# Window attention with one group of 49 tokens per matmul, smaller array tiles and a pair of accumulator banks

## The chip, the cores and the metric

The kernel runs on one core of a Trainium2 chip. A core has five engines with their own instruction streams: TensorE (matrix products; PE in the profile, its weight loads PEld), VectorE (DVE), ScalarE (ACT), GpSimd (POOL) and SyncE (SP, which issues the DMAs here). They meet through semaphores alone. TensorE writes into PSUM, eight banks of 512 fp32 numbers on each of 128 partitions; ScalarE and VectorE carry results from there to SBUF, the working memory. The metric is the device time of one execution in microseconds.

## The reference, cut to what matters

Four layers run over 32 images of 56 x 56 x 96: a conditional convolution block, a 5x5 depthwise convolution with a residual, a 3x3 depthwise with a pointwise convolution and batch norm, and a Swin block (window attention and an MLP). The change touches the attention of the last:

```python
shifted = jnp.roll(x, (-SHIFT, -SHIFT), axis=(1, 2))      # SHIFT = 3
win = _window_partition(shifted)                          # windows of 7 x 7 = 49 tokens
h = _layernorm(win, ln1_g, ln1_b)
q = (h @ wq).reshape(-1, L, NH, d)                        # L = 49, NH = 3, d = 32
k = (h @ wk).reshape(-1, L, NH, d)
v = (h @ wv).reshape(-1, L, NH, d)
attn = jnp.einsum('nqhd,nkhd->nhqk', q, k) / jnp.sqrt(jnp.float32(d))
attn = attn.reshape(B, nW, NH, L, L) + mask[None, :, None]
attn = jax.nn.softmax(attn, axis=-1).reshape(B * nW, NH, L, L)
out = jnp.einsum('nhqk,nkhd->nqhd', attn, v).reshape(-1, L, C)
```

Everything is fp32.

## The kernel before

An image passes four stages: router, conditional, depthwise and swin. Four images are in flight, one in each stage, so that the engines work on different stages side by side. The stages don't issue instructions; they record pieces of work with a `Recorder` (`call`, L292; several calls that must follow each other directly are put in one piece with `together`, L283). `order` (L339) then plays the pieces through a list scheduler: each engine has a queue sorted by a target time, a piece starts when what it needs is done and its buffers are free, and the function `cost` (L165) says how long it takes. `PLAN` and `interleave` (L1486) give the targets. The order found this way is written out, engine by engine, and every engine works through its list in that order. On the hardware nothing of the costs is left but this order. All recorded instructions carry the line L500 in the profile, since `give` issues them there.

A `Ring` (L194) is a set of equal buffers. The eight PSUM banks are one ring, `mm`, shared by all stages; a piece that needs a new bank waits in the plan until one is free, and a bank is free again when its last user is done. Where TensorE has nothing ready, `order` puts in an idle matmul, `ident` times `ident` (L1504).

In the swin stage an image is cut into 8 rows of windows, of 7 lines x 56 columns = 392 tokens each, that is 8 windows. Two windows that lie side by side make a pack, so a row has `NP` = 4 packs. `kT` and the normalized tokens have 64 columns (`SLOT`) for each window, 49 of them filled; the two windows of a pack lie on partitions 0 to 48 and 64 to 112 once tokens are on partitions, `PS` = 113 rows in all. For row i the loop near L1437 does:

- `exponentials` (L1130): scores of a pack, transposed (keys on partitions), are one product for each head, of 32 x 113 keys with 98 queries. Each head has its own bank and its own 32 rows of the array. All 113 x 98 scores of a pack come out; only the two 49 x 49 blocks on the diagonal belong to one window. ScalarE takes exp of those blocks, one instruction for each head and window of a pack (all four packs at once), into `exps`, whose other blocks were set to zero at the start (L703).
- `kept` (L1159): GpSimd multiplies by 0 or 1 where the shifted windows hold unrelated regions: the last window of a row, and all windows in the last row.
- `averaged` (L1174): sums of the exponentials with a stationary matrix of ones (`ones32`), three products of 113 rows with 392 columns into one bank, one head on each 32 columns of the array; then the products with `v`, one for each pack and head, into a second bank. ScalarE takes Ln of the sums and exp(-Ln) for the reciprocal.
- `divided` (L1202): VectorE refines the reciprocal with one Newton step and multiplies it with the averages. `attended` (L1274) projects the result and adds it to the residual.

The loop runs with a lag: scores of row i stand beside the sums of row i - 1 and the projection of row i - 2. A second version of the kernel for large scores (`general`) stands behind a branch that isn't taken with these inputs.

Of the kernel before, what the change touches and what calls it, by code (L numbers as in the profile page):

```python
# [14 lines left out]
ALU = mybir.AluOpType  # L15
# [149 lines left out]
def cost(engine, method, args, kw):  # L165
    if method == "preload_act_table_set":
        return 1300
    out = kw["out"] if "out" in kw else args[0]
    n = math.prod(out.shape[1:])
    if engine == "tensor":  # L170
        if method == "transpose":
            return 127
        k, m = args[1].shape[0], math.prod(args[1].shape[1:])
        if k == 32 and m == 32:
            return 68 * n / 392
        if k == 32:
            return 86
        if m == 32:
            return 75 if n < 128 else 255
        return 195 if n < 128 else 80 + 1.6 * n  # L180
    if len(args) > 3 and args[3] == ALU.pow:
        return 200 + 200 * n
    fixed, each = COST[engine, method]
    if engine == "scalar":
        if kw.get("accum_out") is not None:
            fixed += 190
        if hasattr(kw.get("scale"), "shape"):
            each += 0.37 if hasattr(kw.get("bias"), "shape") else 0.23
        elif hasattr(kw.get("bias"), "shape"):
            each += 0.25  # L190
    return fixed + each * n


class Ring:  # L194


    def __init__(self, tiles, banks=False):
        self.tiles, self.banks = tiles, banks
        self.free = [(0.0, n) for n in range(len(tiles))]
        self.made = self.begun = 0  # L200


class Buffer:


    def __init__(self, ring):
        self.ring = ring
        self.number = ring.made
        ring.made += 1
        self.slot = None  # L210
        self.users = {}
        self.state = {}
        self.owner = None


class View:
# [25 lines left out]
        return View(self.buffer, self.shown, self.path, parts)  # L242

    def found(self):
        t = self.buffer.ring.tiles[self.buffer.slot]
        for name, args, kw in self.path:
            t = getattr(t, name)(*args, **kw)
        return t
# [12 lines left out]
class Recorder:  # L261
# [23 lines left out]
        yield  # L285
        self.open = None

    def new(self, ring):
        b = Buffer(ring)
        return View(b, ring.tiles[0])  # L290

    def call(self, engine, method, args, kw, reads=(), writes=()):  # L292
        marks = (kw.pop("reads", ()), kw.pop("writes", ()))
# [45 lines left out]
    def order(self):  # L339
# [26 lines left out]
        def available(w):  # L366
            need = {}
            for b in w.needs:
                if b.slot is None:
                    need.setdefault(b.ring, []).append(b.number)  # L370
            return all(
                len(n) <= len(ring.free) and (ring.banks or max(n) < ring.begun + len(n)) for ring, n in need.items()
            )

        running = {}

# [11 lines left out]
        def done(w, now):  # L388
            for b in w.uses:
                b.left -= 1  # L390
                if not b.left:
                    b.ring.free.append((now, b.slot))
            for v in w.after:
                v.waits -= 1
                lag = 0 if v.engine == w.engine else TO_TENSOR[w.engine] if v.engine == "tensor" else CROSSING
                v.ready = max(v.ready, now + lag)
                if not v.waits:
                    ready.append(v)
# [6 lines left out]

        def begin(w):
            nonlocal count
            for b in w.needs:
                if b.slot is None:
                    b.ring.free.sort()  # L410
                    b.slot = b.ring.free.pop(0)[1]
                    b.ring.begun += 1
            result.append(w)
            w.start = now
            e = w.engine
            if e == "gpsimd" or e == "vector" and w.calls[0][0] == "scalar_tensor_tensor":
                running[e] = {"work": w, "left": w.ns, "since": now, "rate": 1.0}
                share(now)
                return
            free[e] = now + w.ns  # L420
            heapq.heappush(events, (free[e], count, None))
            heapq.heappush(events, (free[e] + w.landing, count + 1, w))
            count += 2
            if e == "tensor":
                heapq.heappush(events, (free[e] + SPARE_AFTER, count, None))
                count += 1
# [77 lines left out]
def kernel(  # L504
# [10 lines left out]
    def ring(name, shape, n):  # L515
        return Ring([const.tile(shape, F32, name=f"{name}{k}") for k in range(n)])

    def banks(name, n):
        return Ring([psum.tile([P, 512], F32, name=f"{name}{k}") for k in range(n)], banks=True)

    mm = cv = banks("banks", 8)
    xTs = ring("xT", [C, H * W], 2)
    h2s = ring("h2", [P, NB, STRIP * W], 2)
    wmixs = ring("wmix", [C, M], 2)
# [164 lines left out]
    else:  # L689
# [2 lines left out]

        slots = ring("slots", [C, NWIN, SLOT], 3)

        exps = ring("exps", [P, NH, NP, PK], 2)
        ones32 = const.tile([P, HD], F32, name="ones32")

    def first_others():
        for t, src in held:
            nc.sync.dma_start(out=t, in_=src)  # L700
        if not general:
            for t in slots.tiles + kTs.tiles + exps.tiles:
                nc.gpsimd.memset(t, 0.0)  # L703
            nc.gpsimd.memset(ones32, 1.0)

# [371 lines left out]
    def stage_swin(b, res):  # L1077
# [52 lines left out]
        def exponentials(i):  # L1130
# [2 lines left out]
            pss = [chip.new(mm) for _ in range(NH)]  # L1133
            with chip.together():
                for j in range(NP):
                    for h in range(NH):
                        hs = slice(h * HD, (h + 1) * HD)
                        chip.tensor.matmul(
                            pss[h][:PS, j * PK : (j + 1) * PK],
                            kT[hs, 2 * SLOT * j : 2 * SLOT * j + PS],  # L1140
                            qT[hs, j * PK : (j + 1) * PK],
                            start=True,
                            stop=True,
                        )
            e = exps_of[i] = chip.new(exps)
            for h in range(NH):
                for at in range(2):
                    ks, qs = slice(SLOT * at, SLOT * at + WT), slice(WT * at, WT * at + WT)
                    chip.scalar.activation(
                        e[ks, h, :, qs].part((h, at)),  # L1150
                        pss[h][ks, :RT].rearrange("k (j q) -> k j q", j=NP)[:, :, qs],
                        AF.Exp,
                        scale=1.0 / math.sqrt(HD),
                        reads=(tables,),
                    )

        every = [(h, at) for h in range(NH) for at in range(2)]

        def kept(i):  # L1159
            e = exps_of[i]  # L1160
            if i < NROW - 1:
                ks = slice(SLOT, PS)
                view = e[ks, :, NP - 1, WT:].part(*((h, 1) for h in range(NH)))
                chip.gpsimd.tensor_tensor(
                    view, view, keep_column[ks, None, :].to_broadcast([WT, NH, WT]), ALU.mult
                )
                return
            for at in range(2):
                ks = slice(SLOT * at, SLOT * at + WT)
                for h in range(NH):  # L1170
                    view = e[ks, h, :, WT * at : WT * at + WT].part((h, at))
                    chip.gpsimd.tensor_tensor(view, view, keep_last[ks], ALU.mult)

        def averaged(i):  # L1174

            v = rows_of.pop(i)[2]
            e = exps_of.pop(i).part(*every)
            pd = chip.new(mm)
            with chip.together():
                for h in range(NH):  # L1180
                    chip.tensor.matmul(
                        pd[h * HD : (h + 1) * HD, :RT],
                        ones32[:PS],
                        e[:PS, h].rearrange("k j q -> k (j q)"),
                        start=True,
                        stop=True,
                    )
            po = chip.new(mm)
            with chip.together():
                for j in range(NP):  # L1190
                    for h in range(NH):
                        hs = slice(h * HD, (h + 1) * HD)
                        chip.tensor.matmul(
                            po[hs, j * PK : (j + 1) * PK], v[:PS, j, hs], e[:PS, h, j], start=True, stop=True
                        )

            inv = chip.new(hids)[:C, :RT]
            chip.scalar.activation(inv, pd[:C, :RT], AF.Ln, reads=(tables,))
            chip.scalar.activation(inv, inv, AF.Exp, scale=-1.0, reads=(tables,))
            averages[i] = pd, po, inv  # L1200

        def divided(i):  # L1202

            pd, po, inv = averages.pop(i)
            step = chip.new(hids)[:C, :RT]
            chip.vector.tensor_tensor(step, pd[:C, :RT], inv, ALU.mult)
            chip.vector.scalar_tensor_tensor(step, step, 2.0, inv, ALU.subtract, ALU.mult)
            oT = output_of(i)
            chip.vector.tensor_tensor(
                oT[:C].rearrange("c (r n w) -> c r n w", n=NWIN, w=7),  # L1210
                by_windows(step),
                by_windows(po[:C, :RT]),
                ALU.mult,
            )

# [351 lines left out]
```

## Time and profile before

| | |
|---|---|
| time, median of 3 runs | 5202.46 us (5202.14 to 5204.24) |
| profiled execution, span | 5212.6 us |
| granted TensorE clock, mean | 0.985 |
| score matmuls, `banks<-qT,kT` 32x98 | 6144 records, 267.4 us busy |
| sums, `banks<-exps,ones` 113x392 | 1536 records, 221.7 us busy |
| averages, `banks<-exps,v` 113x98 | 6144 records, 221.9 us busy |
| POOL `exps<-exps,keep_column` 49x147 | 224 instructions, 925 ns each |
| DVE `hid<-banks,hid`, `hid<-hid,hid`, `oT<-hid,banks`, 96x392 | 256 each; 555, 637 and 551 ns |
| POOL `tb<-tb` 112x384 | 128 instructions, 1372 ns each |

The profile is of one execution, whose span is 0.2% over the median of the runs. A group is named by what it writes and reads, with partitions x elements; rows with a star give rows*columns of the array that a matmul uses. Each matmul call shows as two weight loads and two matmul records. Busy time of a group of matmuls is the union of overlapping records, so the mean of one record is much longer than its share of the time.

### The profile page before, as it was taken

Reading aid. Unit: us, or ns where it says so; the run is one execution under the profiler, and the core shown is the slowest. Engines: PE = TensorE matmul, PEld = TensorE weight load, DVE = VectorE, ACT = ScalarE, POOL = GpSimd, SP = SyncE. Lnnn points to the kernel's source line nnn. Section 1 sums busy time; section 2 is a strip of 40 time slices with the busy share of each in tenths; the row PEclk is TensorE's granted clock in tenths of the full one; section 3 lists DMA queues with packets and bytes.
Section 4 is the critical chain, followed back from the end, with each engine's and each line's share of the span. In section 5 each row is a group of like instructions: output and inputs, shape, how many; then the busy total and the mean of one; then the engine's idle time right before and its main releaser. Section 6 shows DMA issues by size and latency. Waiting matters only on the chain.

```text
span 5212.6 us, 139630 instructions
## 1 busy us (share of the span) xinstructions
PE 5050.6 (97%) x58578; PEld 3343.9 (64%) x58578; DVE 4300.9 (83%) x5561; ACT 3836.9 (74%) x7649; POOL 3028.8 (58%) x2432
## 2 busy tenths in 40 slices
PE   5789999999999999999999999999999999999999
PEld 4556666666666666666666666666666666666677
DVE  7877988888888888888888888888888888888722
ACT  3457778877778777777877777877777877777755
POOL 5455766565665556666555665656576555566533
PEclk9899999999999999999999999999999999999999
DMA  1111101111111111111111111111111111110110
GB/s 43 23 28 37 38 18 32 33 39 36 39 21 30 31 39 36 39 23 30 33 35 37 37 30 26 30 36 38 37 35 22 32 33 39 36 39 21 23 28 19
DMA packets 482577, 166.34 MB, mean 32 GB/s; under 512 B 477951, under 2 KB 478612, under 8 KB 478868
## 3 DMA queue, kind: packets, MB, share of 16 engines
q1 hardware_dynamic: 481940, 157.33, 14.8%
q8 instruction: 463, 7.59, 0.6%
q14 instruction: 174, 1.43, 0.1%
HBM read 41.60 MB, written 38.54 MB: 15 GB/s over the span
## 4 chain that ended last, share of the span: by engine, by line
PE 74%; POOL 10%; DVE 5%; ACT 5%; issue 4%; DMA 1%; SPq 0%; ACTq 0%; DVEq 0%; POOLq 0%
PE banks L500 74%; DVE h L500 3%; POOL tb L500 3%; POOL lnd L500 2%; POOL xT L500 2%; ACT exps L500 2%; POOL exps L500 2%; POOL var L500 1%; ACT hid L500 1%; ACT h L500 1%; DMA out<-tb 1%; DVE wmix L500 1%; DVE hid L500 1%; ACT slots L500 0%; DVE res L500 0%
## 5 line engine op out<-in xcount | busy, mean ns | idle before, releaser
L500 DVE SCALAR_TENSOR_TENSOR h<-h,mix,h 128x784 f32<-128x784 f32 x3072 | 3309.6, 1113 | 71.1 <-ACT h L500 54.0
L500 POOL TENSOR_TENSOR var<-var,mhalf 112x4 f32<-112x4 f32 (+1 forms) x512 | 775.2, 1519 | 426.3 <-DVE var L500 419.6
L500 PE MATMUL banks<-x,band 32*32 32x392 f32 x24576 | 856.3, 510 | 0.0
L500 POOL TENSOR_TENSOR xT<-y,xT 96x392 f32<-96x392 f32 x256 | 470.2, 1838 | 445.5 <-ACT y L500 444.1
L500 PE MATMUL banks<-xT,wmix 96*128 96x448 f32 (+1 forms) x1536 | 697.9, 553 | 0.5 <-DVE wmix L500 0.5
L500 ACT ACTIVATE h<-h,biasd,s 128x784 f32<-128x784 f32 x384 | 398.9, 1039 | 366.1 <-DVE h L500 366.0
L500 ACT ACTIVATE hid<-banks,c 128x448 f32<-128x448 f32 (+1 forms) x768 | 436.5, 582 | 288.3 <-PE banks L500 279.9
L500 POOL TENSOR_TENSOR tb<-res 112x384 f32<-112x384 f32 (+1 forms) x256 | 476.4, 1866 | 286.7 <-DMA out<-tb 196.7
L500 PEld LDWEIGHTS banks<-w,hid 128*112 128x112 f32 x5376 | 584.7, 183 | 82.0 <-issue 37.8
L500 PE MATMUL banks<-hT,w 96*128 96x448 f32 (+1 forms) x1536 | 615.6, 502 | 0.2 <-DVE tb L500 0.2
L500 POOL TENSOR_TENSOR lnd<-res,var 112x384 f32<-112x384 f32 (+1 forms) x512 | 594.8, 1168 | 32.8 <-PE banks L500 16.2
L500 ACT ACTIVATE h<-banks,bias,s 128x448 f32<-128x448 f32 (+1 forms) x768 | 538.6, 709 | 91.0 <-PE banks L500 85.4
L500 PE MATMUL banks<-w,hid 128*112 128x96 f32 x5376 | 593.1, 267 | 7.4 <-ACT hid L500 6.4
L500 PE MATMUL banks<-h,wmix 128*96 128x392 f32 x1536 | 557.7, 501 | 15.7 <-ACT h L500 15.7
L500 PEld LDWEIGHTS banks<-x,band 32*32 32x32 f32 x24576 | 404.7, 103 | 250.9 <-issue 165.9
L500 ACT ACTIVATE exps<-banks 49x196 f32<-49x196 f32 x1536 | 506.2, 330 | 40.2 <-PE banks L500 15.3
L500 POOL TENSOR_TENSOR exps<-exps,keep_column 49x147 f32<-49x147 f32 x224 | 207.1, 925 | 480.8 <-ACT exps L500 427.4
L500 PEld LDWEIGHTS banks<-h,wmix 128*96 128x96 f32 x1536 | 244.1, 165 | 256.8 <-issue 209.2
L500 PEld LDWEIGHTS banks<-xT,wmix 96*128 96x128 f32 x1536 | 261.2, 192 | 200.7 <-issue 95.5
L500 DVE TENSOR_REDUCE var<-lnsq 112x4 f32<-112x388 f32 (+1 forms) x512 | 253.1, 497 | 157.6 <-POOL lnd L500 118.1
L500 ACT ACTIVATE h<-h,mix 128x784 f32<-128x784 f32 x384 | 364.5, 949 | 18.0 <-POOL h L500 10.1
L500 PEld LDWEIGHTS banks<-hT,w 96*128 96x128 f32 x1536 | 256.4, 190 | 144.9 <-issue 74.8
(132 smaller groups left out, 7460.2 us busy)
## 6 DMA issues: line engine op xcount, KB each, us to landing
xT<-in_x SPq DMA_DIRECT2D x32, 1176.0 KB
x<-xT SPq DMA_DIRECT2D x384, 98.0 KB
out<-tb SPq DMA_DIRECT2D x128, 168.0 KB
filtered<-x SPq DMA_DIRECT2D x384, 49.0 KB
filtered<-x SPq DMA_DIRECT2D x384, 42.0 KB
out<-tb SPq DMA_DIRECT2D x128, 126.0 KB
filtered<-x SPq DMA_DIRECT2D x384, 7.0 KB
wpw<-in_L_conv_Wpw SPq DMA_DIRECT2D x1, 576.0 KB
```

The costliest lines, as they stand in the source:

```text
L500: getattr(getattr(self.nc, w.engine), method)(*args, **kw)
```

## The change

The scores and averages are made for one window at a time. Scores: the stationary operand is the 64 columns of `kT` of one window and one head, the moving one its 49 queries; the window's place in its pack, `at`, gives the half of the partitions that the result goes to. `exps` no longer has blocks that are never used: it is 128 partitions x 3 heads x 4 packs x 49, so exp is one instruction for each head over all 128 partitions (rows 49 to 63 and 113 to 127 hold what the zero columns of `kT` give). In the last row `kept` is one multiplication over all heads.

```diff
             with chip.together():
                 for j in range(NP):
-                    for h in range(NH):
-                        hs = slice(h * HD, (h + 1) * HD)
-                        chip.tensor.matmul(
-                            pss[h][:PS, j * PK : (j + 1) * PK],
-                            kT[hs, 2 * SLOT * j : 2 * SLOT * j + PS],
-                            qT[hs, j * PK : (j + 1) * PK],
+                    for at in range(2):
+                        n = 2 * j + at
+                        for h in range(NH):
+                            hs = slice(h * HD, (h + 1) * HD)
+                            chip.tensor.matmul(
+                                pss[h][SLOT * at : SLOT * (at + 1), j * WT : (j + 1) * WT],
+                                kT[hs, SLOT * n : SLOT * (n + 1)],
+                                qT[hs, WT * n : WT * (n + 1)],
...
             e = exps_of[i] = chip.new(exps)
             for h in range(NH):
-                for at in range(2):
...
+                chip.scalar.activation(
+                    e[:, h].rearrange("k j q -> k (j q)").part(h),
+                    pss[h][:, : NP * WT],
+                    AF.Exp,
...
+            keep = keep_last.rearrange("k j q -> k (j q)")
+            view = e.rearrange("k h j q -> k h (j q)")
+            chip.gpsimd.tensor_tensor(view, view, keep[:, None, :].to_broadcast([P, NH, NP * WT]), ALU.mult)
```

Sums and averages of a row go into one pair of neighbouring banks, one bank for each half of the partitions: columns 0 to 195 hold the sums, 256 to 451 the averages. All thirty products are one piece of work. Their outputs are written in the order line, pack, column, in runs of 7.

```diff
-            pd = chip.new(mm)
...
-            po = chip.new(mm)
...
+            both = chip.new(mm, pair=True)
+            halves = [slice(SLOT * at, SLOT * at + WT) for at in range(2)]
+            with chip.together():
+                for at, ks in enumerate(halves):
+                    for h in range(NH):
+                        chip.tensor.matmul(
+                            both[h * HD : (h + 1) * HD, at, : NP * WT].rearrange("c (r j w) -> c j r w", j=NP, w=7),
+                            ones32[ks],
+                            e[ks, h].rearrange("k j q -> k (j q)"),
...
                 for j in range(NP):
+                    for at, ks in enumerate(halves):
+                        for h in range(NH):
+                            hs = slice(h * HD, (h + 1) * HD)
+                            chip.tensor.matmul(
+                                both[hs, at, 256 : 256 + NP * WT].rearrange("c (r j w) -> c j r w", j=NP, w=7)[:, j],
+                                v[ks, j, hs],
+                                e[ks, h, j],
...
-            chip.scalar.activation(inv, pd[:C, :RT], AF.Ln, reads=(tables,))
+            chip.scalar.activation(inv, both[:C, :, : NP * WT], AF.Ln, reads=(tables,))
```

`divided` reads both banks in one instruction and puts the two halves side by side as it writes `oT`. The eight banks are now allocated as four tensors of two banks. The ring gives a pair only where an even bank and the next one are free together, gives single banks first from pairs that are already broken, and serves a pair ahead of single banks in the same piece. The memset of `exps` is gone.

```diff
+    def room(self, buffers):
+        twice = sum(b.pair for b in buffers)
+        if len(buffers) + twice > len(self.free):
+            return False
+        if twice and twice > len(self.halves()[1]):
+            return False
+        return self.banks or max(b.number for b in buffers) < self.begun + len(buffers)
...
+        slots = {n for _, n in self.free}
+        alone = [f for f in self.free if f[1] ^ 1 not in slots] if self.pairs else []
+        f = (alone or self.free)[0]
...
-    mm = cv = banks("banks", 8)
+    pairs = [psum.tile([P, 2, 512], F32, name=f"banks{k}") for k in range(4)]
+    mm = cv = Ring([pairs[k // 2][:, k % 2] for k in range(8)], banks=True, pairs=pairs)
```

`cost` gets planned times for the new products, in ns for a call:

```diff
+        if k == 32 and m == SLOT:
+            return 28
+        if k == WT:
+            return 24 if n == WT else 60
         if k == 32:
             return 86
         if m == 32:
-            return 75 if n < 128 else 255
+            return 75
```

## The prediction

> **What bounds the kernel now.** I read the page first (busy shares and the chain), then the table of two-image windows, then the groups with shapes kept apart, then one stretch of TensorE's timeline. The page:
>
> ```profile
> PE 5050.6 (97%) x58578; PEld 3343.9 (64%) x58578; DVE 4300.9 (83%) x5561; ACT 3836.9 (74%) x7649; POOL 3028.8 (58%) x2432
> ...
> PE   5789999999999999999999999999999999999999
> ...
> DVE  7877988888888888888888888888888888888722
> ...
> PE 74%; POOL 10%; DVE 5%; ACT 5%; issue 4%; DMA 1%; SPq 0%; ACTq 0%; DVEq 0%; POOLq 0%
> ```
>
> In the two rows of digits each digit is the busy tenths of a fortieth of the span. TensorE is busy nearly throughout, VectorE at eight to nine tenths until the last two slices, where only the last image's attention is left; and three quarters of the chain that ends last lie on it. A busy TensorE can hide waiting, because ends are modelled and because the plan puts in idle matmuls (`ident` times `ident`) where nothing is ready. So the steady part has to be looked at. The work repeats every 310 us, two images:
>
> ```profile
> core 0: us, PE busy (x) PEld busy (x) DVE busy (x) ACT busy (x) POOL busy (x), PEclk, DMA share, GB/s
> 1200.00:1510.00 310.00, 306.02 (x3595) 199.83 (x3595) 268.97 (x344) 238.91 (x478) 185.13 (x151) 0.99 0.16 33
> 2400.00:2710.00 310.00, 306.04 (x3596) 200.32 (x3594) 268.75 (x344) 238.89 (x478) 184.52 (x151) 0.99 0.16 33
> ```
>
> TensorE leaves 4 of 310 us free (2 us an image); VectorE leaves 41, ScalarE 71, GpSimd 125. In the window 600 to 4700 us, 26.5 images, the idle matmuls number few:
>
> ```profile
> L500 PE MATMUL banks<-ident 128*128 128x128 f32 x524 | 81.8, 283 | 0.0
> ```
>
> 524 records, about 119 ns from start to start, are 62 us or 2.4 us an image. So of 155 us for an image TensorE has 150 us of needed work, and saved TensorE time should shorten the period until VectorE (134 us an image) is full.
>
> One row (56 x 7 tokens, 8 rows an image, 256 in all) spends this on attention products; the columns are start and duration in us:
>
> ```profile
> 2526.69 1.04 PE L500 MATMUL banks<-qT,kT 32*113 32x98 f32 x24
> 2527.67 0.86 PE L500 MATMUL banks<-exps,ones 113*32 113x392 f32 x6
> 2528.35 0.86 PE L500 MATMUL banks<-exps,v 113*32 113x98 f32 x24
> 2529.14 0.53 PE L500 MATMUL banks<-wo,oT 97*112 97x97 f32 x3
> ```
>
> Start to start: scores 0.98, sums 0.68, averages 0.79, together 2.45 us. Each call appears as two records (fp32 passes). Three tiles, one per head, work side by side, so scores and averages are 8 rounds of three and the sums 2 rounds. The single records behind these rows show rounds starting 99.3 ns apart in the scores, 84.5 in the averages and 329 in the sums; inside a round, tiles start about 7 ns apart. 329/392 is 0.84 ns a column, and 98 columns of it are 82 of the 84.5: the averages and sums stream columns. The scores' 99.3 is more than 82; that is their weight load of 113 columns. What is left of a group (0.98 less 8 x 99.3, 0.79 less 8 x 84.5) is 0.19 and 0.11 us for filling and for the drain where the next group has another tile shape.
>
> **What the Trainium skill says.** "TensorEngine Tiling (Array Packing)", Tiling Modes: 32x64 gives 8 tiles, 64x32 also 8, tiles load and multiply in parallel, and a change of mode drains the engine. The trace agrees for 32x113, 113x32 and for 12 tiles of 32x32; the two new shapes are not in it. "TensorE: Matmul & The Clock Gate", LDWEIGHTS: a load costs its columns/1.2 ns, whatever the contraction. 113/1.2 is 94 ns beside the 99.3 ns round: agrees. The same page, "Wait — 56ns, not 53.3ns?": start-to-start never drops below about 25 ns. The 7 ns between tiles contradicts this within a burst; for a long run the fastest in the trace is 84.5/3 = 28 ns a pair, so it stays open. "PSUM — Partial Sum Buffer", Specifications: a non-contiguous output slows matmuls significantly. Every output before is contiguous, so no row shows it.
>
> **The change part by part.**
>
> Scores (L1130): 12 calls of 113x98 become 24 of 64x49, six tiles at once (three heads, two column halves), so still 8 rounds. A round is the larger of the load, 64/1.2 = 53 plus the 5 seen above = 58 ns, the stream 49 x 0.84 = 41, and six starts, 42. 8 x 58 + 0.19 = 0.65 us: saves 0.33.
>
> Sums (L1174): 3 calls over 392 columns become 6 over 196, six tiles at once (two row halves into two banks): 2 x 196 x 0.84 plus 0.02 = 0.35 us: saves 0.33.
>
> Averages: 12 calls become 24, 8 rounds of six. Load 32/1.2 = 27, stream 41 + 3, starts 42: I take 48 ns. 8 x 48 + 0.11 = 0.49: saves 0.30. Outputs of sums and averages now go out in runs of 7 words. I price this at nothing, since an fp32 pass writes only one element per 0.84 ns; the other end is a doubling, which takes back 0.33 and 0.35 and leaves the scores' 0.33.
>
> TensorE sum: I round 0.96 down to 0.88 us a row, for skew not seen in the trace. 256 x 0.88 = 225 us, 7.0 us an image. Ends: 0.96 x 256 = 246, and with slow scattered writes 0.28 x 256 = 72.
>
> ScalarE: six exponentials of 49x196 become three of 128x196.
>
> ```profile
> L500 ACT ACTIVATE exps<-banks 49x196 f32<-49x196 f32 x1536 | 506.2, 330 | 40.2 <-PE banks L500 15.3
> L500 POOL TENSOR_TENSOR exps<-exps,keep_last 49x196 f32<-49x196 f32 x192 | 170.2, 909 | 64.8 <-ACT exps L500 60.7
> L500 ACT ACTIVATE x<-banks 128x392 f32<-128x392 f32 x192 | 80.9, 494 | 27.1 <-PE banks L500 27.1
> L500 ACT ACTIVATE hid<-banks 96x392 f32<-96x392 f32 x256 | 126.3, 493 | 21.5 <-PE banks L500 17.9
> ```
>
> The last two rows: 128 and 96 partitions cost the same, so I keep 330 ns. 768 x 330 = 253 us leave ScalarE, 0.99 us a row, and the scores' three banks come free that much earlier.
>
> GpSimd: `kept` for a last row is one multiply of 128x588 for six of 909 ns. `tb<-tb` 112x384 takes 1372, so 588/384 of it is 2.1 us (ends 1.7 and 2.9): 3.4 us x 32 = 107 us less, on a wait that the sums sit behind. The other rows' 49x147 stays.
>
> VectorE: three operations a row at 392 elements stay (555, 637, 551 ns); only their patterns change. The last one already reads permuted runs of 7 at the price of the contiguous one, so nothing is added.
>
> Waits: the sums and averages become one unit, so Ln waits for all 30 calls. It began 0.68 us after the group's start and will begin about 0.84 after: 0.16 us on the path to the division, hidden behind other rows' ScalarE work; uncovered, it would cost 0.16 x 256 = 41 us. The bank of the sums is now held until the last VectorE operation, some 1.7 us longer (637 + 551 + Exp). And an even/odd pair of banks must be free at one moment; everything queued for a bank on TensorE can stand behind that. No DMA and nothing in SP's queue is changed. The planner's constants for the new calls change the order written out for all engines; I give that no value of its own, but an uncertainty below.
>
> Total: the period goes from 155 by at most 7.0 to 148; VectorE's 134 is then 91% of it, so VectorE is what is late next, and I take off a tenth: 6.3 us x 32 images = 202 us, and 3 us for the end, where the last image runs alone and its row chain is shorter by the exponentials. The profiled span is 5212.6 us and nothing lies around it in the times shown; their median 5202.46 is 0.998 of it. 5212.6 - 205 = 5007.6, x 0.998 = 4998 us.
>
> **The rivals.**
>
> A, forecast (0.64): 4998, own range 4945 to 5060.
>
> B, partial (0.24): another limit takes over early. Either scattered writes are slow (72 us of TensorE left) or pairs of banks come late and VectorE at 91% can't be kept fed, with idle matmuls growing from 2.4 to about 6 us an image. Then about 95 us remain: 5107, with 0.03 of the chance within 0.2% of before. For it: GpSimd and VectorE hold 15% of the chain. Against it: only 4 us of gaps in 310.
>
> C, slower (0.12): long runs of small tiles hit an issue floor. At the page's 25 ns a pair scores and averages take 96 x 25 = 2.4 us plus 0.3 for fill and drain plus 0.35 for the sums, 3.05 us against 2.45: +0.6 us x 256 = 154 us, 5356. It decides from (2.45 - 0.65)/96 = 19 ns a pair upward. For it: nothing in the trace runs faster than 28 ns a pair for long, and calls double. Against it: each rate seen is already explained by columns or loads, and six records in a burst start within 15 ns.
>
> That the tiles don't run in parallel at all would look like C, only stronger.
>
> **How the numbers follow.** The predicted time is A's. The range 4945 to 5130 holds A, most of B, and leaves out C and the ends. Taking 0.2% (10 us) as what can be told from no change: faster 0.85 (A and most of B), within it 0.03, slower 0.12.
>
> **What would show it.** Matmul records rise by 27 calls x 2 x 256 = 13824. Right: groups of 48 score records about 0.65 us start to start, 12 sum records 0.35, 48 average records 0.5; 768 exponentials at 330 ns; a two-image period near 297 us. Wrong for sizes: averages at 0.8 us (slow writes). C: 48 records at 1.2 us or more. B: small groups as forecast, but more `ident` records and gaps, the period above 303.

## The result, and the profile after

The changed kernel takes 6101.7 us (median of 4 runs, 6070.35 to 6122.49) against 5203.2 us of the kernel before on the same chip: ratio 1.172, 95% interval 1.1685 to 1.1758. 4998 was predicted. The profiled execution has a span of 6068.5 us at a mean granted clock of 0.951 (before: 5212.6 and 0.985).

The page of the changed kernel, the lines that answer to those shown of before:

```profile
PE 5354.7 (88%) x73354; PEld 3485.9 (57%) x73354; DVE 4245.9 (70%) x5561; ACT 3585.7 (59%) x6881; POOL 2892.8 (48%) x2270
...
PE   5788888898899899989888988889998899888898
...
DVE  7856867676777677677767677676766876777612
...
PE 44%; ACT 9%; DVE 5%; issue 3%; POOL 2%; DMA 0%; ACTq 0%; SPq 0%; DVEq 0%; POOLq 0%
```

ScalarE's work fell by 251 us and GpSimd's by 136, as meant, and yet each engine of the page is busy for a smaller share of the span. TensorE's row of digits has eights where it had nines from end to end. TensorE's busy time rose by 304 us although its work shrank, and its idle time rose from 162 to 714 us (span less busy).

Part of this is the clock. In the traces it is either full or half. It is half for 595 us of the changed kernel's profile and for 162 us of the one before, and TensorE is slower there: records of `banks<-h,wmix` start 653 ns apart at half clock and 329 elsewhere, in both. So up to 217 of the 898 us may be a slower TensorE (half of 433 us; an estimate, and an upper end, since TensorE doesn't set the pace everywhere). No run isolates what lowers the clock.

The two 310 us windows that held exactly two images before:

```profile
core 0: us, PE busy (x) PEld busy (x) DVE busy (x) ACT busy (x) POOL busy (x), PEclk, DMA share, GB/s
1200.00:1510.00 310.00, 281.29 (x4131) 176.22 (x4130) 227.62 (x287) 195.31 (x380) 154.36 (x121) 1.00 0.15 32
2400.00:2710.00 310.00, 274.82 (x3501) 182.97 (x3501) 223.05 (x288) 187.20 (x361) 158.38 (x122) 0.93 0.16 32
```

TensorE now leaves 29 and 35 us of 310 free, where it left 4. VectorE gets through 287 instructions in place of 344. The two windows are no longer alike: the strict repeat of two images is gone.

Were the new matmuls slower than thought? Two stretches of TensorE's timeline, start and duration in us, in brackets the idle time before and what ended it:

```profile
2545.12 0.90 PE L537 MATMUL banks<-slots,wq 96*96 96x392 f32 x2 [0.31 <-ACT h L537]
...
2583.58 0.77 PE L537 MATMUL banks<-qT,kT 32*64 32x49 f32 x48
2584.28 0.88 PE L537 MATMUL banks<-ident,lnd 112*96 112x112 f32 x7
2584.99 0.40 PE L537 MATMUL banks<-ident 128*128 128x128 f32 x2
2585.32 0.55 PE L537 MATMUL banks<-exps,ones 49*32 49x196 f32 x12
2585.68 0.66 PE L537 MATMUL banks<-exps,v 49*32 49x49 f32 x48
2586.27 0.59 PE L537 MATMUL banks<-ident,lnd 112*96 112x112 f32 x4
...
2588.56 0.90 PE L537 MATMUL banks<-slots,wq 96*96 96x392 f32 x2 [0.76 <-ACT h L537]
2589.94 0.90 PE L537 MATMUL banks<-slots,wk 96*96 96x392 f32 x2 [0.48 <-ACT exps L537]
```

They were not. Start to start, the scores take 0.70 us, the sums 0.36, the averages 0.59: 1.65 us against 2.45. What is new are the brackets, on projections to queries and keys. The profile says what ended a wait, not why it was waited for. The compiled program does: each instruction names the semaphore values that it waits for, and these can be traced back to the instruction that sets them. The last two lines wait until the bank that they write has been read by its last user; these are true waits, for a bank that comes late. The first line waits for an activation that reads the other bank of its tensor, and shares no data with it. Over 600 to 4700 us the table of TensorE's waits (total us, times, longest) had two lines before:

```profile
PE banks L500 <- POOL lnd L500: 44.3, 39, 2.8
PE banks L500 <- ACT hid L500: 6.4, 13, 0.5
```

Now it is much longer and begins with

```profile
PE banks L537 <- ACT h L537: 90.4, 120, 2.4
PE banks L537 <- ACT hid L537: 53.9, 80, 1.4
PE banks L537 <- ACT y L537: 33.0, 46, 2.2
PE banks L537 <- ACT res L537: 29.6, 44, 3.4
PE banks L537 <- ACT exps L537: 27.4, 59, 1.1
```

Many short waits; the largest totals are on ScalarE operations, which carry results out of banks. In the same window the idle matmuls, which were 524 records, are

```profile
L537 PE MATMUL banks<-ident 128*128 128x128 f32 x1144 | 200.7, 306 | 58.0 <-ACT h L537 20.9 <-DVE res L537 11.3 <-ACT slots L537 5.5
```

and the pieces that were to shrink on the other engines did:

```profile
L537 ACT ACTIVATE exps<-banks 128x196 f32<-128x196 f32 x768 | 211.0, 331 | 142.5 <-PE banks L537 129.7 <-POOL var L537 3.9 <-DVE res L537 3.2
...
L537 POOL TENSOR_TENSOR exps<-exps,keep_last 128x588 f32<-128x588 f32 x32 | 50.3, 1571 | 23.2 <-ACT exps L537 13.8 <-PE banks L537 9.5
```

So every local effect came, and the kernel lost 898 us. Two things had changed for the whole program besides the attention products: how the banks are allocated, and the order written out.

### The profile page after: what moved, and what is told of

It reads as the page before. It is cut to its first block, busy times and chain, and to the rows that moved or that the text cites. A ratio compares the mean times of both kernels' runs of the same rounds, so it can differ in the third digit from the quotient of the medians.

```text
span 6068.5 us, 167841 instructions
## 1 busy us (share of the span) xinstructions
PE 5354.7 (88%) x73354; PEld 3485.9 (57%) x73354; DVE 4245.9 (70%) x5561; ACT 3585.7 (59%) x6881; POOL 2892.8 (48%) x2270
## 4 chain that ended last, share of the span: by engine, by line
PE 44%; ACT 9%; DVE 5%; issue 3%; POOL 2%; DMA 0%; ACTq 0%; SPq 0%; DVEq 0%; POOLq 0%
PE banks L537 44%; DVE h L537 3%; ACT h L537 3%; ACT hid L537 2%; DVE hid L537 1%; DVE res L537 1%; POOL var L537 1%; ACT slots L537 1%; ACT exps L537 1%; ACT y L537 1%; POOL lnd L537 0%; ACT x L537 0%; DVE tb L537 0%; ACT res L537 0%; POOL tb L537 0%
## 5 line engine op out<-in xcount | busy, mean ns | idle before, releaser
L537 DVE SCALAR_TENSOR_TENSOR h<-h,mix,h 128x784 f32<-128x784 f32 x3072 | 3253.0, 1093 | 249.8 <-ACT h L537 236.2
L537 POOL TENSOR_TENSOR var<-var,mhalf 112x4 f32<-112x4 f32 (+1 forms) x512 | 825.3, 1616 | 792.7 <-DVE var L537 717.7
L537 PE MATMUL banks<-x,band 32*32 32x392 f32 x24576 | 885.4, 511 | 25.1 <-ACT h L537 10.2
L537 PE MATMUL banks<-xT,wmix 96*128 96x448 f32 (+1 forms) x1536 | 734.0, 578 | 72.1 <-ACT h L537 15.3
L537 PE MATMUL banks<-hT,w 96*128 96x448 f32 (+1 forms) x1536 | 646.1, 517 | 113.1 <-ACT hid L537 44.0
L537 PE MATMUL banks<-ident 128*128 128x128 f32 x2624 | 424.7, 300 | 149.2 <-ACT h L537 65.6
L537 POOL TENSOR_TENSOR tb<-res 112x384 f32<-112x384 f32 (+1 forms) x256 | 356.0, 1395 | 370.6 <-DMA out<-tb 274.6
L537 PEld LDWEIGHTS banks<-ident 128*128 128x128 f32 x2624 | 362.7, 204 | 245.3 <-ACT h L537 83.5
L537 DVE TENSOR_TENSOR tb<-banks,tb 112x384 f32<-112x384 f32 (+1 forms) x256 | 129.6, 506 | 469.6 <-PE banks L537 330.3
L537 DVE TENSOR_TENSOR hid<-banks,hid 96x392 f32<-96x392 f32 x256 | 142.6, 557 | 395.7 <-ACT hid L537 361.1
```

The lines of the kernel that those rows point to most:

```text
L537: getattr(getattr(self.nc, w.engine), method)(*args, **kw)
```

## The experiments

Times are medians; each ratio is against the kernel before on the same chip, with its 95% interval. "Single tensors" means eight tensors of one bank, as before; "wide tensors" four of two banks, as in the change.

### The tensors alone

The kernel before, same order, same bank numbers, same instructions, with one edit:

```diff
-        return Ring([psum.tile([P, 512], F32, name=f"{name}{k}") for k in range(n)], banks=True)
...
+    pairs = [psum.tile([P, 2, 512], F32, name=f"banks{k}") for k in range(4)]
+    mm = cv = Ring([pairs[k // 2][:, k % 2] for k in range(8)], banks=True)
```

> The kernel before with one edit: the eight banks are allocated as four tensors of two banks, as in the changed kernel; the planned order and every bank's number stay the same. Theory W (waits are drawn for a whole tensor, so a matmul into one bank also waits for readers and writers of its neighbour): far slower, 5700 to 6600 us, with TensorE gaps of several hundred us. Rival L (the choice of just-freed banks makes the waits): 5203 +- 10 us. Rival P (late pairs of banks): 5203 +- 10 us.

Measured: 5853.54 us, 1.1247 (1.1227 to 1.1267). No planned operation differs, nor does the bank of any, and 647 us are lost. Its page and its waits of TensorE:

```profile
PE 5362.9 (92%) x58578; PEld 3423.2 (58%) x58578; DVE 4254.7 (73%) x5561; ACT 3861.0 (66%) x7649; POOL 2936.3 (50%) x2432
```

```profile
PE banks L500 <- ACT exps L500: 46.0, 71, 1.2
PE banks L500 <- ACT h L500: 44.7, 58, 1.9
PE banks L500 <- ACT hid L500: 31.8, 53, 1.7
PE banks L500 <- ACT slots L500: 27.0, 46, 1.9
```

The same list of waits on ScalarE is here. The record counts are those of before (58578), yet busy time rose by 312 us, and idle time by 328. This profile is at half clock for 442 us in place of 162, which is up to 140 us of the busy time (an estimate); the rest may be waiting between a record that has begun and the next, which would count as busy, and is not separated here. The compiled programs show why TensorE waits. Its waits on ScalarE, traced back to the instruction that sets the semaphore:

```
kernel                               the other end uses
                                     the same bank   the other bank of the two
before                                    2662                0
before with wide tensors                   299             1945
changed kernel                             906             1106
changed kernel in single tensors          2481                0
```

Counted are the waits that a matmul carries itself; a wait for data that the matmul reads is not put into the second column. The last row is the program of the next run. The semaphores are drawn for a whole tensor. A matmul into one bank of a pair waits for whoever still reads the other bank, and the reader of one bank for a matmul that fills the other (1363 waits of ScalarE in the wide kernel, none before). These are false waits: no data is shared. With the program's waits laid over the profiles, matmuls that wait for the other bank alone have 328 of the 490 us of TensorE's idle time in front of them in the wide kernel, and 312 of the 714 us in the changed one. There another 247 us stand before matmuls that wait for their own bank alone (44 of 162 us before).

### The change with its waits made true

The changed kernel's own order and bank numbers, in single tensors. An instruction that spans the pair (logarithm, first and last division) is written out once for each bank:

```diff
-    pairs = [psum.tile([P, 2, 512], F32, name=f"banks{k}") for k in range(4)]
-    mm = cv = Ring([pairs[k // 2][:, k % 2] for k in range(8)], banks=True, pairs=pairs)
+    mm = cv = Ring([psum.tile([P, 512], F32, name=f"banks{k}") for k in range(8)], banks=True, pairs=[None])
...
+                    if w.engine != "tensor" and any(v.buffer.pair for v in views):
+                        for at in range(2):
```

> The changed kernel with its own planned order and bank numbers, but eight tensors of one bank; the three instructions that read both banks of a pair (Ln, first and last VectorE operation) are written out as two each, one for each bank, without the planner's knowledge (some 150 ns more on ScalarE and 300 ns on VectorE a row). Theory W (waits on the neighbour's bank): 5350 to 5550 us, the loss from 5203 to 6102 falls by more than half. If those waits don't matter in this order: 6100 us or more.

Measured: 5483.34 us, 1.0526 (1.0503 to 1.0549). 618 of the 898 us go with the false waits, although the split may itself cost something (below). And the changed kernel, still wide, with the rule dropped that gives a single bank from a broken pair first:

```diff
-        alone = [f for f in self.free if f[1] ^ 1 not in slots] if self.pairs else []
-        f = (alone or self.free)[0]
+        f = self.free[0]
```

> The changed kernel, four tensors of two banks and pairs, but a single bank is the longest free one, no longer one whose neighbour is in use. Theory W: still 5700 to 6100 us, since every bank has a neighbour to wait for. Rival L (the choice of banks makes the loss): 5400 us or less.

Measured: 5759.97 us, 1.1064 (1.1045 to 1.1082). 342 us better than the change, still wide: the rule hands out the neighbour of a bank in use, with which false waits are surest. This run also has a new order, so it is not as clean as the first. The rule alone, on the kernel before with its single tensors:

```diff
-                    b.slot = b.ring.free.pop(0)[1]
+                    slots = {n for _, n in b.ring.free}
+                    alone = [f for f in b.ring.free if f[1] ^ 1 not in slots] if b.ring.banks else []
+                    f = (alone or b.ring.free)[0]
```

> The kernel before with one edit: a new bank is taken first from banks whose neighbour is in use, no longer the one that has been free longest; eight tensors of one bank, no pairs. In the plan 11% of the banks are then taken again within 300 ns of their release, for 2% before (14% in the changed kernel). Theory W: within 1% of 5203 us. Rival L: 5500 to 6100 us, the larger part of the change's loss. Rival P: 5203 us.

Measured: 5174.94 us, 0.9949 (0.9932 to 0.9967). In the plan this rule makes 11% of the banks be reused within 300 ns of their release (2% before, 14% in the change). The rival that quick reuse costs time falls: with true waits the time fell by half a per cent, at a granted clock of 0.992 for 0.987.

### Other ways to hold the results

If false waits were all, single banks would give back the whole forecast. Three ways were run: two independent single banks in place of a pair; the same without idle matmuls; and one dedicated pair beside six single tensors.

```diff
-            both = chip.new(mm, pair=True)
+            both = [chip.new(mm) for _ in range(2)]
```

> The changed kernel, but sums and averages of the two halves go into any two single banks (eight tensors of one bank, the longest free taken first); Ln, the first and the last VectorE operation of the division become two instructions each, one for each bank. Theory W: the waits are gone, faster than before by less than forecast since the plan has 1247 idle matmuls for 836: 5000 to 5150 us. Rival L: the same, since the oldest bank is taken. Rival I (the small tiles themselves disturb other work on the chip): 5700 us or more.

Measured: 5459.81 us, 1.0485 (1.0459 to 1.0510). Some 300 us above the range of Theory W.

```diff
-    chip.spare = ident, ident, mm
+    chip.spare = None
```

> The version with two single banks and the new planned times, without any idle matmul (they compute nothing that is used). If the idle matmuls are what eats the saved time: 5150 to 5250 us. Theory F: little change, 5350 to 5550 us, since the waits stay and merely move; a lower TensorE clock if gaps are what lowers it.

Measured: 5448.66 us, 1.0486 (1.0450 to 1.0522). Leaving the idle matmuls out gains nothing as a whole: TensorE's busy time falls from 5139 to 4961 us, but the granted clock falls from 0.954 to 0.926, with 811 us at half clock for 509. The two may cancel; whether the idle matmuls cost anything at an equal clock stays open.

```diff
+    mm = cv = Ring([psum.tile([P, 512], F32, name=f"banks{k}") for k in range(6)], banks=True)
+    twins = Ring([psum.tile([P, 2, 512], F32, name=f"wide{k}") for k in range(1)], banks=True)
...
-            both = chip.new(mm, pair=True)
+            both = chip.new(twins)
```

> The changed kernel, but the pair for sums and averages is one tensor of its own and the other six banks are six tensors of one bank, the longest free taken first. All instructions of the attention are those of the changed kernel. Theory W: no wait on a stranger's bank, 5030 to 5200 us, some lost because six banks serve the rest (11% of banks taken again within 300 ns in the plan). Rival L: as much slower as that share says, 5400 us or more. Rival I: 5700 us or more.

Measured: 5380.69 us, 1.0330 (1.0313 to 1.0348), above the range of Theory W again. Here TensorE waits most for the one pair (`wide`): its longest total is for the last division, `oT`, of the row that still holds it.

```profile
PE wide L537 <- DVE oT L537: 85.7, 38, 3.9
PE banks L537 <- DVE res L537: 18.1, 14, 2.5
```

### The order alone

The planner writes the order of all engines from planned times, and the change gave it new ones for its matmuls. So the old times were put back into two of the versions above (43, 37.5 and 127.5 ns a call, which add up to what the larger calls were planned at):

```diff
-            return 28
+            return 43
...
-            return 24 if n == WT else 60
+            return 37.5 if n == WT else 127.5
```

> The version with two single banks, and one more edit: the planner is told for the new products the times that the old ones had (43, 37.5 and 127.5 ns for a call, so that a row is planned as long on TensorE as before); the idle matmuls go from 1247 back to 862. Theory F (the planned order is what fails now: told of the saving, the planner writes an order of the same length with more idle matmuls and earlier reuse of banks, and the chip then waits in it): 5050 to 5200 us. Rival I (the new instructions themselves disturb the chip): as the version with two single banks, 5460 us.

Measured with two single banks: 5307.47 us, 1.0189 (1.0164 to 1.0214): 152 of the 253 us come back from numbers that reach no instruction, but less than expected.

> The version with a pair of its own, with the old planned times for the new products. Its plan is 1.4% longer than that with the new times (5470 for 5390 planned us). Theory F: 5100 to 5300 us, faster than the 5381 of the new times. Rival I: 5381 us or more.

Measured with the dedicated pair: 5337.41 us, 1.0252 (1.0235 to 1.0269): 43 us better than with the new times, but above the expected range as well. Then the other way round, the kernel before with nothing changed but what the planner is told about the attention products:

```diff
         if k == 32:
-            return 86
+            return 56
         if m == 32:
-            return 75 if n < 128 else 255
+            return 48 if n < 128 else 120
```

> The kernel before, its instructions and its eight single-bank tensors, with one edit: the planner is told shorter times for the old attention products (56, 48 and 120 ns for a call, what the new ones of the same row are given). Theory F: slower than before although no instruction is another, 5300 to 5600 us. Rival I: 5203 us within 1%.

Measured: 5578.33 us, 1.0734 (1.0716 to 1.0752). Seven per cent from the order, with what the order does to the clock (0.969 for 0.987) in it. Is it that times which are too short make a bad order? The same edit with times 5% longer (90, 79 and 267):

> The kernel before, the planner told of 5% longer attention products (90, 79 and 267 ns for 86, 75 and 255). Nothing else is changed. Theory R: 5300 us or more, as with shorter times. Theory F (shorter planned times make the order too tight): 5200 us within 1%, or faster, as the plan gets more room, though it is 1.8% longer in planned time.

Measured: 5443.19 us, 1.0460 (1.0443 to 1.0478). So it is not a matter of sign: both other orders that the planner wrote for these instructions lose. Part of what they lose to is seen in TensorE's waits of the last run (before: `lnd` 44.3 us in 39 waits, longest 2.8):

```profile
PE banks L500 <- POOL lnd L500: 122.0, 41, 11.9
PE banks L500 <- POOL exps L500: 16.3, 22, 5.8
```

About as many waits on `lnd`, but up to 12 us long. (The clock is lower too, 0.971 for 0.986.) If GpSimd is planned too fast, telling the planner that it takes 27% longer should help:

```diff
+    if engine == "gpsimd":
+        return 1.27 * (fixed + each * n)
```

> The version with two single banks and the new times, and the planner told of 1.27 times longer GpSimd instructions (3.03 ms in all, as the profile before has it, for 2.39 planned). Theory G (TensorE waits behind GpSimd's normalizations because the plan takes GpSimd for faster than it is): 5100 to 5300 us, waits of TensorE on lnd and exps down by half. Theory R (the order before is a rare good one, and any other order costs some per cent): 5350 to 5550 us.

Measured on the version with two single banks: 5386.44 us, 1.0337 (1.0319 to 1.0355). 73 us better than without, and still slower than before. TensorE's waits on `lnd` and `exps` were not halved, as Theory G expects: 99.5 us between 600 and 4700 us, for 103.6 without the edit. So this is one more draw of an order rather than a repair.

### The small matmuls under the order of before

What is left open is whether the small matmuls save anything. To hold the order, the kernel before got the small scores only, planned at the same total, so that the plan is the same to the instruction and to the bank:

```diff
                 for j in range(NP):
+                    for at in range(2):
+                        n = 2 * j + at
...
-                            pss[h][:PS, j * PK : (j + 1) * PK],
+                                pss[h][SLOT * at : SLOT * (at + 1), WT * n : WT * (n + 1)],
```

> The kernel before with its order, its banks and every other instruction unchanged; only the scores are made as in the changed kernel: 24 small matmuls (64 x 49) for a group of rows in place of 12, planned at the same 43 units so that the written order stays the same. On TensorE this saves 0.27 us of 0.98 in each of 256 score groups, 70 us in all. Theory A/R (the small tiles save time as far as TensorE sets the pace, and it is the new order and the wide tensors that lose): 5130 to 5160 us, ratio 0.986 to 0.992. Rival N (the other engines and the order hide it, TensorE merely waits longer): 5193 to 5213 us. Rival I (the small matmuls cost something elsewhere): above 5220 us.

Measured: 5184.12 us, 0.9953 (0.9939 to 0.9966). A gain, between the two theories: 24 us of the 70. Page and waits of TensorE:

```profile
PE 4986.6 (96%) x64722; PEld 3284.4 (63%) x64722; DVE 4303.7 (83%) x5561; ACT 3832.5 (74%) x7649; POOL 3063.8 (59%) x2432
```

```profile
PE banks L502 <- POOL lnd L502: 35.7, 26, 2.5
PE banks L502 <- POOL exps L502: 17.8, 26, 1.0
PE banks L502 <- ACT slots L502: 11.7, 26, 0.5
```

TensorE's busy time fell by 64 us and the span of the profile by 30. Some of this is the clock: 112 us at half clock for 162, up to 25 us (an estimate). The times say the same. The 18 executions of the kernel before beside the last experiment below go from 5193.5 us at a clock of 0.989 to 5213.0 at 0.985, 4 to 5 us for each 0.001; the small scores ran at 0.989 and the kernel before beside them at 0.986, so 12 to 15 of the 24 us go with the clock (an estimate). Whether the small scores raise it is not shown. Where saved TensorE time goes is seen in the waits: for the multiplications that clear unrelated regions (`exps`, not in the table before) and for ScalarE's `slots`, 26 waits each in a window of 26.5 images, so about one an image. All waits in that window add up to 77.6 us, for 50.7 before. With the bank rule that had gained by itself:

> The same small scores, with the bank choice of the run that took the neighbour of a bank in use first (5174.94 us). Theory A/R: the two gains add, 5100 to 5145 us, ratio 0.980 to 0.989, faster than both kernels. Rival N: 5165 to 5185 us, as without the small scores. Rival I: above 5190 us.

Measured: 5159.09 us, 0.9907 (0.9892 to 0.9922). This lies between the ranges of the two theories. The two gains add up, nearly, the clock's part included (0.992 for 0.986).

Last, small sums and averages too, in the 131 of 256 rows in which the plan of before happens to leave both banks free for long enough, the logarithm and two divisions written once a bank; and beside it a control with only that split:

```diff
+            for at in range(2):
+                nc.scalar.activation(
+                    inv.found().rearrange("c (j a q) -> c a j q", j=NP, a=2)[:, at],
+                    tile_of((pd, po)[at])[:C, :n].rearrange("c (j q) -> c j q", j=NP),
```

> As the small scores under the unchanged order (5184.12 us), and in the 131 of 256 rows in which the two banks of the averages are both free from the sums to the last division in the unchanged order, sums and averages too are made as in the changed kernel: window by window, into two single banks, with the logarithm, the first and the last division written once for each bank. TensorE saves a further 0.33 + 0.20 to 0.30 us in each of these rows, 70 to 82 us; ScalarE gets 131 x 0.16 = 21 us more, VectorE some 20 us. Theory R (the order loses, the small matmuls gain): about 0.4 of the saving comes out as with the scores, less up to 15 us for the split: 5145 to 5185 us, and below the split-alone kernel by 20 to 50 us. Rival I (sums and averages in small pieces cost time by themselves, which is what is left of the loss of the changed kernel with single banks): above 5215 us and not below the split-alone kernel.

> The control: small scores, order unchanged, sums and averages as before, but the logarithm, the first and the last division of the same 131 rows written in two halves. Theory R: 5184 to 5210 us, the price of the split, 0 to 25 us. Rival I: the same, since it puts the loss on the small sums and averages. If it is above 5230 us, the split itself is a large part of what the changed kernel with single banks loses.

Measured: 5210.5 us, 1.0009 (1.0001 to 1.0018), for the small products; 5223.71 us, 1.0033 (1.0021 to 1.0045), for the split alone. The first stands above its range, and the second above what Theory R expects and below the 5230 from which the split would be a large part of the loss. The busy times of the two pages, small products first:

```profile
PE 4964.0 (95%) x68652; PEld 3297.4 (63%) x68652; DVE 4295.2 (83%) x5823; ACT 3828.6 (74%) x7780; POOL 3117.7 (60%) x2432
PE 5008.0 (96%) x64722; PEld 3301.5 (63%) x64722; DVE 4292.9 (82%) x5823; ACT 3832.2 (73%) x7780; POOL 3137.8 (60%) x2432
```

The difference, 13 us, is less than the 20 to 50 expected but has the sign of a gain, at nearly equal clocks (0.983 and 0.984): the small sums and averages don't lose time by themselves. Of the 44 us that TensorE's busy time fell between the two, 30% came out. The split stands 40 us above the small scores alone, for 131 rows; at 0.984 for 0.989, 20 to 28 us of that go with the clock by the estimate above.

## Why the prediction was wrong

**Matmuls, right.** Scores 0.70 us against 0.65 forecast, sums 0.36 against 0.35, averages 0.59 against 0.49. The saving is 0.80 us a row against the 0.88 used, 205 us against 225. The averages carry the miss: with the 0.11 us for filling and drain that the prediction gives, a round of six takes 60 ns, not 48. Records rose by 14776: the 13824 forecast and 952 more idle ones (2624 against 1672).

**ScalarE and GpSimd, right.** 768 exponentials at 331 ns; 251 us less against 253. `keep_last` takes 1571 ns, below the 1.7 to 2.9 us given, so that its group lost 120 us of work (170.2 to 50.3) and not 107; GpSimd as a whole lost 136.

**Rival C, wrong in its mechanism.** Its side came true, by luck, and its cause did not: 0.70 us for 48 records is 14.6 ns from record to record, below the 19 from which it would decide. "TensorE: Matmul & The Clock Gate" of the Trainium skill, section "Wait — 56ns, not 53.3ns?", gives about 25 ns as the least; these runs contradict it for small tiles side by side. Nor did scattered outputs slow anything visibly, which "PSUM — Partial Sum Buffer", Specifications, had made a doubt. With runs of 7 words the changed kernel takes 356 ns for a row's sums and 594 for its averages, start to start; the run with the small products under the old order, which writes them contiguously, takes 368 and 593 (medians at full clock).

**Waits, the step that failed.** Under "Waits" the prediction counted the later logarithm and "an even/odd pair of banks must be free at one moment". It took the pair for a question of when two banks are free. The line of the diff that allocates all eight banks as four tensors was not priced at all, though it changes the dependencies of every matmul, attention or not. That line alone costs 647 us under the old order, and taking it back gives 618 us under the new, in each case with the change of the clock that comes with it. Rival B named pairs of banks, but as a partial loss of the gain (5107), and by their availability.

**The order, mis-sized.** "I give that no value of its own, but an uncertainty" was worth 2 to 7%: the seven versions of the change with single tensors or a dedicated pair run at 1.019 to 1.053, and the unchanged instructions of before under two other orders at 1.046 and 1.073. The range of 4945 to 5130 had no room for that. What is left of the change's loss after the false waits is 280 us in the run that has them out, with the split's price in it. In size a new order can account for it, since two new orders of unchanged instructions lost 236 and 375 us. A lower clock has a part: that run is at half clock for 562 us in place of 162, up to 200 us (an estimate), more than the reordered kernels with their 311 and 319. Under the order of before the small matmuls don't lower the clock (0.989 with the scores, 0.983 and 0.984 with and without the small products). No run separates the two in the change's own order.

**What a saved TensorE microsecond is worth, mis-sized.** "I take off a tenth" rested on VectorE at 91%. With order and tensors held, 13 of 44 us came out for sums and averages (0.30), at nearly equal clocks and with VectorE at 83%. For the scores it was 24 of 64 (0.38), but about half of the 24 goes with the clock. The plan sits close on GpSimd and ScalarE at particular places in each image, and a TensorE that arrives earlier waits there, as the waits of the run with small scores show. The page's shares of busy time (58% and 74% before) don't show that; the count of waits per image does. At 0.3 the whole saving of 205 us would have been worth some 60 us, an estimate from that ratio; ScalarE's 251 us could not be tried apart, since fewer exponentials make another plan.

Open: why the order of before is so much better than its neighbours. Long waits for GpSimd are shown in the slower ones; which decision of the planner brings them about is not. What lowers the clock in the slower versions is open as well.

## What to carry to other kernels

Allocate accumulator banks as one tensor each unless one instruction must span two, and then make only that pair wide: where semaphores are drawn for a tensor, a wide one ties strangers together. A profile then shows many short waits, but a late bank makes such waits too; the semaphore values in the compiled program, traced back to who sets them, tell the one from the other. In a kernel whose order is written out statically, an edit to any planned time is a change of the whole program: measure it alone, with no instruction changed, before crediting or blaming the edit beside it. Price saved time on the busiest engine by a run with the order held, not by the share of busy time, and put the granted clocks beside small differences before crediting an edit with them.

## What was not expected of the hardware

- Over a group of 48 records, filling and drain included, matmuls in small tiles start every 14.6 ns (32x64, 49 columns, six tiles at once) or 12.4 ns (49x32), each with a weight load of its own.
- In the first 320 us of the profile of before, one operation on GpSimd, `xT<-y,xT`, takes up to 32.9 us (median 1.34) and `lnd` up to 10.6 (median 0.83). From 600 to 4700 us `lnd` takes at most 4.8 us there; in the run with 5% longer planned times it reaches 11.5 us in that stretch, and TensorE's longest wait for it is 11.9 us.
- The granted clock is full or half. Taking the idle matmuls out lowered its mean from 0.954 to 0.926 and left the time where it was (5459.81 and 5448.66 us).
